# Block attention with a residual LayerNorm: three batch groups, 32-column matmul tiles, and a LayerNorm finish moved from VectorE to GpSimd and TensorE

## The chip, the cores and the metric

One core of one Trainium2 chip. The metric is the device time of one execution, in microseconds, taken as the median of several runs.

## The reference

x is 8 batches of 512 rows of 1024 float32 values (4096 rows, 16 MB). Wk and Wo are 1024 x 1024 float32 (4 MB each). Cut to what matters:

```python
block = x.reshape(8, 8, 64, 1024).sum(2)             # 8 blocks of 64 rows in each batch
keys  = einsum('bnh,kh->bnk', block, Wk)             # 64 keys of 1024
keys  = keys / sqrt(mean(keys**2) + 1e-6) * rms_w
att   = softmax(einsum('bnh,h->bn', keys, cond[1]))  # over the 8 blocks of a batch
attended = einsum('bn,bnh->bh', att, block)          # one vector of 1024 per batch
y     = x + (attended @ Wo.T)[:, None, :]            # the same vector for all 512 rows of a batch
out   = x + (y - mean(y)) / sqrt(var(y) + 1e-6) * gamma + beta
```

The projection of a batch needs the sums over all of that batch's rows, so no row can be finished before the whole of its batch has been read.

## The kernel before, in words

**Layout.** Row r of x lies on partition r // 32, so every partition holds 32 rows of one batch, and a batch has 16 partitions. x is read once, in 16 tiles of two rows per partition (1 MB each, SP queue, L158), and stays in SBUF until it is stored.

**Weights.** Wk and Wo come first, in eight 1 MB tiles that take eight of the 16 x buffers (L127). TensorE transposes them in 128 x 128 pieces (L142) into PSUM, and VectorE and ScalarE take turns at copying the result to `wkT` and `woT` (L149, L151).

**Block sums.** VectorE adds the 32 rows of each partition into `acc` (L161, L164): one addition of 128x1024 per row.

**Attention.** `h_major` (L170) multiplies pieces of `acc` with a block-diagonal matrix, which brings h to the partitions and gives each block two columns. `project` (L180) multiplies that with `wkT`: 16 matmuls of 512 columns, stationary operand 128 columns wide. The profile shows each float32 matmul as two instructions. Scores, softmax and weights follow in a chain of small instructions (L199 to L228). `h_major` and `project` run once more, on the attention weights and `woT`, and leave `proj` in PSUM, on every partition the row of its batch.

**LayerNorm.** For each tile of two rows `stats` makes y = x + proj with its row sum (VectorE, L240), the negative mean `nmu` (VectorE, L245), the sum of squares (ScalarE, L249), and 1 / sqrt by the table's square root and a Newton step of small GpSimd instructions (L95 to L105). `finish` makes z = (y + nmu) * gamma into PSUM (VectorE, L258), x = z * rstd + x (VectorE, L262), x = x + beta (GpSimd, L263), and stores the tile (SP queue, L264). So each row has three VectorE instructions, one ScalarE instruction and one GpSimd instruction of 128x1024.

**Order.** The loops only state the work. A planner gives each engine one fixed order: it plays the program through with its own costs, takes the ready instruction that was stated first, and gives a buffer of a pool to the next tile of that tag when an earlier tile has been released. On the chip each engine then works through its own list in that order.

Of the kernel before, what the change touches and what calls it, by code (L numbers as in the profile page):

```python
# [27 lines left out]
def block_attn_resid_kernel(  # L28
# [42 lines left out]

    def block_diag(name, size, inside, outside):
        t = const.tile([P, P], F32, tag=name, name=name)
        nc.gpsimd.memset(t, inside)
        v = t.rearrange("p (g i) -> p g i", i=size)
        nc.gpsimd.affine_select(
            out=v, in_=v, pattern=[[-size, P // size], [0, size]],
            compare_op=ALU.is_ge, fill=outside, base=0, channel_multiplier=1,
        )
        nc.gpsimd.affine_select(  # L80
            out=v, in_=v, pattern=[[size, P // size], [0, size]],
            compare_op=ALU.is_ge, fill=outside, base=size - 1, channel_multiplier=-1,
        )
        return t

    pair = block_diag("pair", P // (B * 8), 1.0, 0.0)
    batch2 = block_diag("batch2", NB, 2.0, 0.0)
    negmask = block_diag("negmask", NB, 0.0, NEG)
# [3 lines left out]
    def inv_sqrt(eng, ssq, n, name):  # L92
        """1 / sqrt(ssq / H + EPS), with one Newton step after the table's square root."""
        v = small.tile([P, n], F32, tag=f"v{n}", name=f"v_{name}")
        eng.tensor_scalar(v, ssq, 1.0 / H, EPS, ALU.mult, ALU.add)  # L95
        s = small.tile([P, n], F32, tag=f"s{n}", name=f"s_{name}")
        nc.scalar.activation(s, ssq, AF.Sqrt, bias=eps_t, scale=1.0 / H)  # L97
        r = small.tile([P, n], F32, tag=f"r{n}", name=f"r_{name}")
        nc.vector.reciprocal(r, s)
        a = small.tile([P, n], F32, tag=f"a{n}", name=f"a_{name}")  # L100
        eng.tensor_tensor(a, r, r, ALU.mult)
        eng.tensor_tensor(a, a, v, ALU.mult)
        eng.tensor_scalar(a, a, -0.5, 1.5, ALU.mult, ALU.add)
        rr = small.tile([P, n], F32, tag=f"rr{n}", name=f"rr_{name}")
        eng.tensor_tensor(rr, r, a, ALU.mult)  # L105
        return rr

# [1 line left out]
    def vec_tile(src, tag, name):  # L109
        t = tmp.tile([P, H], F32, tag=tag, name=name)  # L110
        nc.scalar.dma_start(out=t, in_=src.rearrange("(o h) -> o h", o=1).to_broadcast([P, H]))
        return t

    q_t = vec_tile(cond[LAYER], "t0", "q_t")
    w_t = vec_tile(rms_w, "t1", "w_t")
    qw = bank_pair("qw", "qw")
    nc.vector.tensor_tensor(flat(qw), q_t, w_t, ALU.mult)  # L117
    g_t = vec_tile(gamma, "t0", "g_t")
    gam = bank_pair("gam", "gam")
    nc.scalar.copy(flat(gam), g_t)  # L120
# [181 lines left out]
```

## Time and profile before

| | us |
|---|---|
| median of 3 runs | 257.05 |
| lowest, highest | 256.84, 262.64 |
| span of the profiled execution, first to last instruction | 260.6 |
| VectorE busy | 176.1 |
| GpSimd busy | 93.3 |
| ScalarE busy | 62.9 |
| TensorE busy with matmuls | 61.4 |

The profiled execution is one execution by itself; its time is told by its span of 260.6 us, from the first to the last instruction, with nothing counted around it. That is 3.5 us above the median of the runs and 2.0 us below the slowest of them. PE is TensorE, PEld its loading of the stationary operand, DVE VectorE, ACT ScalarE, POOL GpSimd, SP the engine that issues most transfers. Busy times of engines overlap, so they don't add up to the span. The granted clock of TensorE is given as a share of 2.4 GHz: 1.00 is 2.4 GHz, 0.50 is 1.2 GHz.

### The profile page before, as it was taken

The page shows a single profiled execution, that of the slowest core. Times are in us where ns is not written, and L with a number is a line of the kernel's source. Part 1 is how long each engine was busy: PE and PEld are TensorE (multiplying, and loading weights), DVE is VectorE, ACT ScalarE, POOL GpSimd, SP SyncE. Part 2 cuts the span into 40 slices and gives each one's busy share as a digit, 9 for nine tenths or more (in the row PEclk, how much of TensorE's full clock was granted, in tenths as well). Part 3 has the DMA queues.
Part 4 walks back from the last instruction along what each step waited for, and adds up shares of the span by engine and source line. Part 5 has one row for each costly group of instructions (what it writes and reads, how often), then busy time and mean ns, then how long its engine had stood idle before and what let it go on. Part 6 is the DMA issues. An engine that isn't in the chain of part 4 may idle for free.

```text
span 260.6 us, 1101 instructions
## 1 busy us (share of the span) xinstructions
PE 61.4 (24%) x226; PEld 39.1 (15%) x226; DVE 176.1 (68%) x220; ACT 62.9 (24%) x105; POOL 93.3 (36%) x129
## 2 busy tenths in 40 slices
PE   0518870000008991589800000000000000000000
PEld 0518660000006440444300000000000000000000
DVE  0111549999991003210199999999999999999950
ACT  0123430000000006200068442234443224444000
POOL 6000000000000000000006768776667876666992
PEclk9999997555555899559955555555555555555555
DMA  6999999999300002000000332233332223333254
GB/s 211 418 408 412 423 419 423 423 423 420 128 0 0 0 0 82 0 3 0 0 0 0 161 141 98 86 161 161 161 161 103 98 122 161 161 161 161 89 214 180
DMA packets 7366, 44.11 MB, mean 169 GB/s; under 512 B 704, under 2 KB 704, under 8 KB 3264
## 3 DMA queue, kind: packets, MB, share of 16 engines
q1 hardware_dynamic: 6784, 41.95, 39.3%
q10 hardware_dynamic: 576, 2.10, 2.3%
q8 instruction: 2, 0.03, 0.0%
q14 instruction: 4, 0.03, 0.0%
HBM read 27.26 MB, written 16.78 MB: 169 GB/s over the span
## 4 chain that ended last, share of the span: by engine, by line
DVE 41%; PE 20%; POOL 16%; ACT 8%; issue 7%; DMA 6%; POOLq 1%; ACTq 0%; DVEq 0%
DVE acc L164 14%; POOL x L263 13%; DVE y L240 8%; DVE z L258 7%; DVE x L262 6%; PE proj L180 6%; PE keys L180 6%; PE pt L142 4%; ACT junk L249 4%; DMA w_t<-n_L_cond_rms_weight_dram 3%; DMA g_t<-in_L_cond_ln_gamma_dram 3%; PE p_attT L170 1%; PE p_blkT L170 1%; DVE woT L149 1%; ACT L97 1%
## 5 line engine op out<-in xcount | busy, mean ns | idle before, releaser
L263 POOL TENSOR_TENSOR x<-x,bet 128x1024 f32<-128x1024 f32 x32 | 74.5, 2350 | 1.5 <-issue 0.5
L95 POOL TENSOR_SCALAR v_y<-ssq 128x2 f32<-128x2 f32 x16 | 3.1, 193 | 154.0 <-ACT junk L249 153.9
L249 ACT ACTIVATE junk<-y,nmu 128x1024 f32<-128x1024 f32 x32 | 36.7, 1147 | 82.2 <-DVE nmu L245 76.6
L240 DVE SCALAR_TENSOR_TENSOR y<-x,proj 128x1024 f32<-128x1024 f32 x32 | 37.5, 1204 | 15.9 <-PE proj L180 15.9
L258 DVE SCALAR_TENSOR_TENSOR z<-y,nmu,gam 128x1024 f32<-128x1024 f32 x32 | 40.7, 1277 | 0.0
L262 DVE SCALAR_TENSOR_TENSOR x<-z,rr_y,x 128x1024 f32<-128x1024 f32 x32 | 39.5, 1270 | 0.0
L164 DVE TENSOR_TENSOR acc<-acc,x 128x1024 f32<-128x1024 f32 x30 | 36.8, 1226 | 1.0
L142 PE MATMUL pt<-ident,w 128*128 128x128 f32 x128 | 20.7, 327 | 17.6 <-DMA w<-in_L_cond_Wk_dram 9.3
L142 PEld LDWEIGHTS pt<-ident,w 128*128 128x128 f32 x128 | 18.0, 170 | 20.1 <-issue 9.3
L180 PE MATMUL proj<-woT,attT 128*128 128x512 f32 x32 | 16.5, 680 | 0.7 <-ACT attT L172 0.7
L180 PE MATMUL keys<-wkT,blkT 128*128 128x512 f32 x32 | 15.9, 660 | 0.7 <-ACT blkT L172 0.7
L149 DVE COPY wkT<-pt 128x1024 f32<-128x1024 f32 x4 | 4.9, 1225 | 14.2 <-PE pt L142 14.2
L170 PE MATMUL p_blkT<-pair,acc 128*128 128x128 f32 x16 | 3.8, 429 | 40.3 <-DVE acc L164 40.3
L201 DVE SCALAR_TENSOR_TENSOR kb<-kb,qw 128x512 f32<-128x512 f32 x2 | 1.4, 686 | 16.8 <-ACT kb L199 16.8
L172 ACT COPY blkT<-p_blkT 128x512 f32<-128x512 f32 x1 | 0.6, 586 | 44.7 <-PE p_blkT L170 44.7
L170 PEld LDWEIGHTS p_blkT<-pair,acc 128*128 128x128 f32 x16 | 3.5, 330 | 40.5 <-issue 40.5
L245 DVE TENSOR_SCALAR nmu<-ysum 128x2 f32<-128x2 f32 x16 | 9.2, 575 | 0.0
L180 PEld LDWEIGHTS proj<-woT,attT 128*128 128x128 f32 x32 | 6.9, 220 | 9.7 <-issue 8.8
L180 PEld LDWEIGHTS keys<-wkT,blkT 128*128 128x128 f32 x32 | 6.8, 216 | 9.3 <-issue 8.3
L149 DVE COPY woT<-pt 128x1024 f32<-128x1024 f32 x4 | 4.9, 1224 | 4.7 <-PE pt L142 4.7
L117 DVE TENSOR_TENSOR qw<-q_t,w_t 128x1024 f32<-128x1024 f32 x1 | 1.2, 1232 | 9.6 <-DMA w_t<-n_L_cond_rms_weight_dram 9.6
L249 ACT ACTIVATION_READ_ACCUMULATOR junk<-y,nmu 128x1 f32 x32 | 6.0, 186 | 0.0
(60 smaller groups left out, 59.5 us busy)
## 6 DMA issues: line engine op xcount, KB each, us to landing
x<-in_x_dram SPq DMA_DIRECT2D x16, 1024.0 KB, 19.8
out_dram<-x SPq DMA_DIRECT2D x16, 1024.0 KB, 3.8
w<-in_L_cond_Wk_dram SPq DMA_DIRECT2D x4, 1024.0 KB, 11.6
w<-in_L_cond_Wo_dram SPq DMA_DIRECT2D x4, 1024.0 KB, 17.5
q_t<-in_cond_dram ACTq DMA_DIRECT2D x1, 512.0 KB, 5.6
w_t<-n_L_cond_rms_weight_dram ACTq DMA_DIRECT2D x1, 512.0 KB, 8.2
g_t<-in_L_cond_ln_gamma_dram ACTq DMA_DIRECT2D x1, 512.0 KB, 7.1
bet<-in_L_cond_ln_beta_dram ACTq DMA_DIRECT2D x1, 512.0 KB, 4.3
```

The lines of the kernel that those rows point to most:

```text
L95: eng.tensor_scalar(v, ssq, 1.0 / H, EPS, ALU.mult, ALU.add)
L142: nc.tensor.transpose(pt[:, c, r * P : (r + 1) * P], stage[which, s][:, r, bass.ts(4 * h4 + c, P)], ident,)
L149: nc.vector.tensor_copy(dst, pt)
L164: nc.vector.tensor_tensor(acc, acc, xx[:, r, :], ALU.add)
L170: nc.tensor.matmul(pb[:, c, :], acc[:, bass.ts(c, P)], rhs, start=True, stop=True)
L180: nc.tensor.matmul(po[:, k, :], lhs[:, c, :], wT[:, c, bass.ts(k, HALF)], start=(c == 0), stop=(c == HC - 1),)
L240: nc.vector.scalar_tensor_tensor(y[:, r, :], xt[t][:, r, :], 1.0, proj, ALU.mult, ALU.add, accum_out=ysum[:, r : r + 1],)
L245: nc.vector.tensor_scalar(nmu, ysum, -1.0 / H, None, ALU.mult)
L249: nc.scalar.activation(junk, y[:, r, :], AF.Square, bias=nmu[:, r : r + 1], accum_out=ssq[:, r : r + 1])
L258: nc.vector.scalar_tensor_tensor(flat(z), y[:, r, :], nmu[:, r : r + 1], flat(gam), ALU.add, ALU.mult)
L262: nc.vector.scalar_tensor_tensor(xr, flat(z), rstd[:, r : r + 1], xr, ALU.mult, ALU.add)
L263: nc.gpsimd.tensor_tensor(xr, xr, bet, ALU.add)
```

## The change

x is worked on in three groups of 2, 2 and 4 batches (`GROUPS`). Each group is spread over all 128 partitions, so groups 0 and 1 have 8 rows per partition (4 tiles of 1 MB), group 2 has 16 (8 tiles). x and the weights share 12 buffers in place of 16: the tiles of group 0 are loaded first, then Wk, Wo, group 1, and group 2, whose tiles take buffers as they come free.

Block sums go from VectorE to TensorE: a 32-column block matrix times 512 columns of x, with the two halves of two rows going to the four 32-partition strips of one PSUM bank. Keys and projection use a stationary operand of 32 columns, with four quarters of the 1024 outputs going to the four strips. Every group has its own block sums, keys, softmax and projection; `spread` matmuls bring the projection to all partitions (`pb`), `pick` matmuls make a small table `tab` of gamma, beta and the projections.

The finish of a row is rewritten as out = y * (1 + gamma * rstd) + (nmu * rstd * gamma + beta - proj): ScalarE makes the factor A, GpSimd the product, TensorE the second bracket as outer products of a transposed table `lt` with `tab` (two matmuls of 512 columns, 6 or fewer used rows of the array), and VectorE adds it. y is written over x. Statistics go by four rows (a quad) in place of two, 1 / sqrt by Ln and Exp. All functions used on ScalarE are in one table, loaded at the start.

```diff
-    for t in range(NT):
...
-            for r in range(RT):
-                nc.vector.tensor_tensor(acc, acc, xx[:, r, :], ALU.add)
...
+GROUPS = (2, 2, 4)
+XBUFS = 12
...
+    xp = ctx.enter_context(tc.tile_pool(name="xp", bufs=XBUFS))
+    work = ctx.enter_context(tc.tile_pool(name="work", bufs=2))
...
+    nc.scalar.preload_act_table_set("natural_log_exp_and_others")
...
+    def block_sums(G):
+        bs = ps.tile([P, HALF], F32, tag="bs", name=f"bs{G['n']}")
+        n = G["rows"]
+        for r in range(n):
+            for h in range(2):
+                j = 2 * (r % 2) + h
+                nc.tensor.matmul(
+                    bs[32 * j : 32 * j + 32, :], blk[G["g"]], G["x"][r // RT][:, r % RT, bass.ts(h, HALF)],
+                    start=(r < 2), stop=(r >= n - 2),
+                )
+        G["bs"] = bs
+
+    def project(lhs, wT, name):
+        po = ps.tile([P, QU], F32, tag="sm", name=name)
+        for c in range(HC):
+            for j in range(4):
+                nc.tensor.matmul(
+                    po[32 * j : 32 * j + 32, :], lhs(c), wT[:, c, bass.ts(j, QU)],
+                    start=(c == 0), stop=(c == HC - 1),
+                )
+        return po
...
+    def attend(G):
...
+        nc.scalar.copy(bss, G["bs"])
+        pb = ps.tile([P, HC, 32], F32, tag="sm", name=f"pblk{n}")
+        for c in range(HC):
+            nc.tensor.matmul(pb[:, c, :], bss[:, bass.ts(c % 4, P)], halves[:, c // 4, :], start=True, stop=True)
+        blkT = chain.tile([P, HC, 32], F32, tag="blkT", name=f"blkT{n}")
+        nc.vector.tensor_copy(blkT, pb)
+
+        keys = project(lambda c: blkT[:, c, :], wkT, f"keys{n}")
...
+        nc.scalar.activation(junk, kb, AF.Square, accum_out=sd[:, 0:1])
+        nc.vector.scalar_tensor_tensor(junk2, kb, 1.0, qw, ALU.mult, ALU.mult, accum_out=sd[:, 1:2])
+
+        sdd = small.tile([P, 2, 32], F32, tag="sdd", name=f"sdd{n}")
+        for s in range(2):
+            nc.vector.tensor_scalar(sdd[:, s, :], diag4, sd[:, s : s + 1], None, ALU.mult)
+        pc = ps.tile([P, 2, 32], F32, tag="sm", name=f"pc{n}")
+        nc.tensor.matmul(flat(pc), ones, flat(sdd), start=True, stop=True)
...
+        nc.scalar.activation(r0, pc[:, 0, :NB], AF.Ln, bias=eps_t, scale=1.0 / H)
+        nc.scalar.activation(r0, r0, AF.Exp, scale=-0.5)
+        nc.vector.tensor_scalar(v, pc[:, 0, :NB], 1.0 / H, EPS, ALU.mult, ALU.add)
+        nc.vector.tensor_tensor(a, r0, r0, ALU.mult)
...
+        wb = chain.tile([P, HC, NB], F32, tag="wb", name=f"wb{n}")
+        nc.vector.tensor_tensor(wb, blkT[:, :, :NB], sc.unsqueeze(1).to_broadcast([P, HC, NB]), ALU.mult)
...
+        att = chain.tile([P, HC, g, 32 // g], F32, tag="att", name=f"att{n}", bufs=2)
+        nc.vector.tensor_copy(att, aT.unsqueeze(3).to_broadcast([P, HC, g, 32 // g]))
+        G["att"] = att
+
+    def proj(G):
+        n, g = G["n"], G["g"]
+        att = G["att"]
+        po = project(lambda c: att[:, c].rearrange("p b m -> p (b m)"), woT, f"po{n}")
...
+        nc.scalar.copy(pr, po)
+        pb = ps.tile([P, 4, QU], F32, tag="pb", name=f"pb{n}")
+        for j in range(4):
+            nc.tensor.matmul(pb[:, j, :], spread[:, j, :], pr, start=True, stop=True)
+        pt = ps.tile([P, 2, QU], F32, tag="sm", name=f"ptab{n}")
+        for k in range(2):
+            nc.tensor.matmul(pt[:, k, :], pick[g][:, k, :], pr, start=True, stop=True)
+        tab = chain.tile([P, HALF], F32, tag="tab", name=f"tab{n}", bufs=2)
+        nc.vector.tensor_tensor(tab, flat(pt), rows, ALU.add)
+        G["pb"], G["tab"] = flat(pb), tab
...
+    def front(G, q):
...
+        xs = G["x"][QT * q : QT * q + QT]
+        for r in range(R):
+            xr = xs[r // RT][:, r % RT, :]
+            nc.vector.scalar_tensor_tensor(
+                xr, xr, 1.0, G["pb"], ALU.mult, ALU.add, accum_out=ysum[:, r : r + 1]
+            )
+        nc.gpsimd.tensor_scalar(nmu, ysum, -1.0 / H, 0.0, ALU.mult, ALU.add)
+        for r in range(R):
+            junk = work.tile([P, H], F32, tag="A", name=f"sq{n}_{q}_{r}")
+            nc.scalar.activation(
+                junk, xs[r // RT][:, r % RT, :], AF.Square, bias=nmu[:, r : r + 1], accum_out=ssq[:, r : r + 1]
+            )
...
+        nc.scalar.activation(r0, ssq, AF.Ln, bias=eps_t, scale=1.0 / H)
+        nc.scalar.activation(r0, r0, AF.Exp, scale=-0.5)
+        nc.gpsimd.tensor_scalar(v, ssq, 1.0 / H, EPS, ALU.mult, ALU.add)
+        nc.gpsimd.tensor_tensor(a, r0, r0, ALU.mult)
+        nc.gpsimd.tensor_tensor(a, a, v, ALU.mult)
+        nc.gpsimd.tensor_scalar(a, a, -0.5, 1.5, ALU.mult, ALU.add)
+        nc.gpsimd.tensor_tensor(rs, a, r0, ALU.mult)
...
+        for k in range(QT):
+            st = stat[G["g"]][k]
+            nc.gpsimd.tensor_tensor(
+                st[:, :, :, 0],
+                nmu[:, RT * k : RT * k + RT].unsqueeze(2).to_broadcast([P, RT, 2]),
+                rs[:, RT * k : RT * k + RT].unsqueeze(2).to_broadcast([P, RT, 2]),
+                ALU.mult,
+            )
+            pl = ps.tile([P, P], F32, tag="sm", name=f"pl{n}_{q}_{k}")
+            nc.tensor.transpose(pl, st.rearrange("p r i k -> p (r i k)"), ident)
+            lt = small.tile([P, P], F32, tag="lt", name=f"lt{n}_{q}_{k}")
+            nc.vector.tensor_copy(lt, pl)
+            lts.append(lt)
+        G["st", q] = (rs, lts)
...
+    def back(G, q):
...
+        for r in range(QT * RT):
+            t = QT * q + r // RT
+            xr = G["x"][t][:, r % RT, :]
+            A = work.tile([P, H], F32, tag="A", name=f"A{n}_{q}_{r}")
+            nc.scalar.activation(A, gam, AF.Identity, bias=1.0, scale=rs[:, r : r + 1])
+            nc.gpsimd.tensor_tensor(xr, xr, A, ALU.mult)
+            b = ps.tile([P, 2, HALF], F32, tag=f"b{r % 2}", name=f"b{n}_{q}_{r}")
+            for i in range(2):
+                lo = 32 * (2 * (r % RT) + i)
+                nc.tensor.matmul(
+                    b[:, i, :], lts[r // RT][lo : lo + K, :], G["tab"][lo : lo + K, :], start=True, stop=True
+                )
+            nc.vector.tensor_tensor(xr, xr, flat(b), ALU.add)
+            if r % RT == RT - 1:
+                nc.sync.dma_start(out=G["out_v"][t], in_=G["x"][t])
...
+    load_x(groups[0])
+    load_w(0, wk)
+    load_w(1, wo)
+    late_vectors()
+    block_sums(groups[0])
+    transpose_w(0, wkT)
+    attend(groups[0])
+    transpose_w(1, woT)
+    proj(groups[0])
+
+    todo = [(G, q) for G in groups for q in range(G["tiles"] // QT)]
+    ready = 1
+    load_x(groups[1])
+    block_sums(groups[1])
+    attend(groups[1])
+    pending = []
+    for G, q in todo:
+        if q == 0 and G["n"] > 0:
+            proj(G)
+        if q == 0 and G["n"] + 1 < len(groups) and G["n"] + 1 > ready:
+            ready = G["n"] + 1
+            load_x(groups[ready])
+            block_sums(groups[ready])
+            attend(groups[ready])
+        front(G, q)
+        pending.append((G, q))
+        if len(pending) > 1:
+            back(*pending.pop(0))
+    while pending:
+        back(*pending.pop(0))
```

## Rows read from the trace of the kernel before

**Rows 1.** Page, part 2: 40 equal slices of 6.5 us, each digit a tenth.

```profile
DVE  0111549999991003210199999999999999999950
...
PEclk9999997555555899559955555555555555555555
...
DMA  6999999999300002000000332233332223333254
```

**Rows 2.** Busy by stage: stretch, length, then PE, PEld, DVE, ACT, POOL; clock, DMA, GB/s.

```profile
18.00:38.00 20.00, 15.67 (x107) 13.92 (x108) 7.35 (x6) 9.07 (x9) 0.00 (x0) 1.00 1.02 416
...
38.00:78.00 40.00, 0.28 (x3) 0.05 (x1) 38.65 (x32) 0.00 (x0) 0.00 (x0) 0.56 0.74 307
...
78.00:83.00 5.00, 3.75 (x16) 3.49 (x16) 0.47 (x1) 0.54 (x1) 0.00 (x0) 0.50 0.00 0
...
83.00:99.00 16.00, 15.90 (x32) 6.80 (x32) 0.69 (x1) 0.05 (x1) 0.00 (x0) 0.88 0.00 0
...
99.00:108.00 9.00, 0.77 (x3) 0.50 (x2) 3.89 (x18) 5.91 (x12) 0.00 (x0) 0.78 0.19 59
...
113.00:129.00 16.00, 16.00 (x32) 6.51 (x31) 0.27 (x1) 0.00 (x0) 0.00 (x0) 0.85 0.00 1
...
146.00:254.00 108.00, 0.00 (x0) 0.00 (x0) 104.99 (x132) 35.89 (x65) 81.01 (x99) 0.50 0.35 145
```

**Rows 3.** Groups by line: engine, out<-in, count | busy us, mean ns | idle before, releaser.

```profile
L263 POOL TENSOR_TENSOR x<-x,bet 128x1024 f32<-128x1024 f32 x32 | 74.5, 2350 | 1.5 <-issue 0.5
...
L258 DVE SCALAR_TENSOR_TENSOR z<-y,nmu,gam 128x1024 f32<-128x1024 f32 x32 | 40.7, 1277 | 0.0
...
L262 DVE SCALAR_TENSOR_TENSOR x<-z,rr_y,x 128x1024 f32<-128x1024 f32 x32 | 39.5, 1270 | 0.0
...
L240 DVE SCALAR_TENSOR_TENSOR y<-x,proj 128x1024 f32<-128x1024 f32 x32 | 37.5, 1204 | 15.9 <-PE proj L180 15.9
...
L249 ACT ACTIVATE junk<-y,nmu 128x1024 f32<-128x1024 f32 x32 | 36.7, 1147 | 82.2 <-DVE nmu L245 76.6 <-POOL a_y L102 5.1
...
L102 POOL TENSOR_TENSOR a_y<-a_y,v_y 128x2 f32<-128x2 f32 x16 | 3.1, 197 | 1.3
...
L97 ACT ACT_TABLE_LOAD x2 | 2.6, 1283 | 0.3 <-DVE kss L206 0.3
```

**Rows 4.** Instructions in time order, 129 to 135 us: start, us, engine, line.

```profile
129.15 1.22 DVE L240 SCALAR_TENSOR_TENSOR y<-x,proj 128x1024 f32<-128x1024 f32 x1 [15.88 <-PE proj L180]
...
130.29 1.22 DVE L240 SCALAR_TENSOR_TENSOR y<-x,proj 128x1024 f32<-128x1024 f32 x1
...
132.58 0.17 DVE L245 TENSOR_SCALAR nmu<-ysum 128x2 f32<-128x2 f32 x1
...
132.78 1.15 ACT L249 ACTIVATE junk<-y,nmu 128x1024 f32<-128x1024 f32 x1 [20.23 <-DVE nmu L245]
...
134.05 1.15 ACT L249 ACTIVATE junk<-y,nmu 128x1024 f32<-128x1024 f32 x1
```

**Rows 5.** The same view, 202 to 256 us.

```profile
202.52 4.66 POOL L263 TENSOR_TENSOR x<-x,bet 128x1024 f32<-128x1024 f32 x2
...
206.58 0.63 DVE L245 TENSOR_SCALAR nmu<-ysum 128x2 f32<-128x2 f32 x1
...
210.18 4.66 POOL L263 TENSOR_TENSOR x<-x,bet 128x1024 f32<-128x1024 f32 x2
...
246.39 9.24 POOL L263 TENSOR_TENSOR x<-x,bet 128x1024 f32<-128x1024 f32 x4
```

**Rows 6.** TensorE weight loads of the keys in time order, 84 to 89 us.

```profile
84.97 0.34 PEld L180 LDWEIGHTS keys<-wkT,blkT 128*128 128x128 f32 x1 [0.52 <-issue]
...
88.54 0.19 PEld L180 LDWEIGHTS keys<-wkT,blkT 128*128 128x128 f32 x1 [0.24 <-issue]
```

**Rows 7.** First transposes, in time order.

```profile
9.31 3.65 PE L142 MATMUL pt<-ident,w 128*128 128x128 f32 x16 [9.31 <-DMA w<-in_L_cond_Wk_dram]
```

**Rows 8.** Page, part 6: DMA issues, KB each, median us to landing.

```profile
out_dram<-x SPq DMA_DIRECT2D x16, 1024.0 KB, 3.8
```

More of the change, by code (lines that the diff above doesn't have):

```diff
@@ L79, in block_diag @@
         )
         nc.gpsimd.affine_select(
-            out=v, in_=v, pattern=[[size, P // size], [0, size]],
-            compare_op=ALU.is_ge, fill=outside, base=size - 1, channel_multiplier=-1,
-        )
[L84 to L88, printed above, removed]
-    eps_t = const.tile([P, 1], F32, tag="eps", name="eps_t")
-    nc.gpsimd.memset(eps_t, EPS)
[L92 to L106, printed above, removed]
@@ L109, in vec_tile @@
[L109 to L120, printed above, removed]
+            out=v, in_=v, pattern=[[-s, n] for s, n in pattern], compare_op=ALU.is_ge, fill=0.0,
@@ new lines, in band, with spots @@
+            base=width - 1, channel_multiplier=-1,
+        )
+    def spots(v, pattern, base):
+        nc.gpsimd.affine_select(
+            out=v, in_=v, pattern=pattern, compare_op=ALU.not_equal, fill=1.0, base=base, channel_multiplier=1
+        )
+    blk = {}
+    for g in sorted(set(GROUPS)):
+        t = const.tile([P, 32], F32, tag=f"blk{g}", name=f"blk{g}")
+        nc.gpsimd.memset(t, 1.0)
+        band(t, [[-(16 // g), 32]], 16 // g)
+        blk[g] = t
+    halves = const.tile([P, 2, 32], F32, tag="halves", name="halves")
@@ new lines, in block_attn_resid_kernel, with late_vectors @@
+    nc.gpsimd.memset(rows, 0.0)
+    def late_vectors():
+        nc.scalar.dma_start(out=gam, in_=gamma.rearrange("(o h) -> o h", o=1).to_broadcast([P, H]))
+        for k, v in ((0, gamma), (1, beta)):
+            h = v.rearrange("(i o h) -> i o h", i=2, o=1)
+            for q in range(4):
+                nc.scalar.dma_start(out=rows[32 * q + k : 32 * q + k + 1, :], in_=h[q % 2])
+    xf = x.rearrange("b s h -> (b s) h")
+    of = out.rearrange("b s h -> (b s) h")
+    groups = []
+    at = 0
@@ new lines, in block_attn_resid_kernel, with load_x @@
+    for n, g in enumerate(GROUPS):
+        lo, hi = at * S, (at + g) * S
+        groups.append(dict(
+            n=n, g=g, rows=4 * g, tiles=4 * g // RT,
+            x_v=xf[lo:hi].rearrange("(p t r) h -> t p r h", p=P, r=RT),
+            out_v=of[lo:hi].rearrange("(p t r) h -> t p r h", p=P, r=RT),
+        ))
+        at += g
+    def load_x(G):
+        G["x"] = []
+        for t in range(G["tiles"]):
+            xx = xp.tile([P, RT, H], F32, tag="x", name=f"x{G['n']}_{t}")
+            nc.sync.dma_start(out=xx, in_=G["x_v"][t])
+            G["x"].append(xx)
@@ L184, in project @@
         return po
-    blkT = h_major(pair, "p0", "blkT")
-    keys = project(blkT, wkT, "p1", "keys")
-    wk_stack.close()
-    late = ctx.enter_context(tc.tile_pool(name="late", bufs=1))
-    bet = late.tile([P, H], F32, tag="bet", name="bet")
-    nc.scalar.dma_start(out=bet, in_=beta.rearrange("(o h) -> o h", o=1).to_broadcast([P, H]))
-    kb = tmp.tile([P, 2, HALF], F32, tag="t0", name="kb")
-    ssq2 = small.tile([P, 2], F32, tag="ssq2", name="ssq2")
-    dot2 = small.tile([P, 2], F32, tag="dot2", name="dot2")
@@ L198, in block_attn_resid_kernel @@
-    for k in range(2):
-        nc.scalar.copy(kb[:, k, :], keys[:, k, :])
-        nc.scalar.activation(keys[:, k, :], keys[:, k, :], AF.Square, accum_out=ssq2[:, k : k + 1])
-        nc.vector.scalar_tensor_tensor(
-            kb[:, k, :], kb[:, k, :], 1.0, qw[:, k, :], ALU.mult, ALU.mult,
-            accum_out=dot2[:, k : k + 1],
-        )
-    kss = small.tile([P, 1], F32, tag="kss", name="kss")
-    nc.vector.tensor_tensor(kss, ssq2[:, 0:1], ssq2[:, 1:2], ALU.add)
-    dot = small.tile([P, 1], F32, tag="dot", name="dot")
@@ L208, in block_attn_resid_kernel @@
-    nc.vector.tensor_tensor(dot, dot2[:, 0:1], dot2[:, 1:2], ALU.add)
-    rrms = inv_sqrt(nc.vector, kss, 1, "keys")
-    score = small.tile([P, 1], F32, tag="score", name="score")
-    nc.vector.tensor_tensor(score, dot, rrms, ALU.mult)
-    diag = const.tile([P, P], F32, tag="diag", name="diag")
-    nc.vector.tensor_scalar(diag, ident, score, None, ALU.mult)
-    pbc = ps.tile([P, P], F32, tag="p0", name="pbc")
-    nc.tensor.matmul(pbc, ones, diag, start=True, stop=True)
-    sm = const.tile([P, P], F32, tag="sm", name="sm")
```

193 lines of the change are left out of this document (98 added, 95 removed).

## The prediction

> **What bounds the kernel now.** I read the profile from the outside in: the slices of the page, the busy times by stage, then single instructions. The slices show four phases one behind the other: transfers alone, VectorE full, VectorE nearly empty, VectorE full to the end [rows 1]. The stages put numbers to it [rows 2]. Until about 38 us the weights load and are transposed at 416 GB/s. From 38 to 78 VectorE is busy 38.65 of 40 us with the row sums. From 78 to 129 the attention runs with little beside it: 3.75 us for the block sums, 15.9 for the keys, 9 for the softmax chain, 16 for the projection. From 129 VectorE streams the rows; it is busy 104.99 of 108 us between 146 and 254, GpSimd 81.01. One row costs it three instructions (1.204, 1.277 and 1.270 us [rows 3]), and a tile of two rows takes 210.18 - 202.52 = 7.66 us [rows 5], 3.83 a row. The last GpSimd addition ends at 246.39 + 9.24 = 255.63, and the span of 260.6 has a tail of 5.0 us behind it, the last store with 3.8 us of it [rows 5, 8]. So the path is loads, row sums, attention, streaming, in series; nothing of the last three lies beside another.
>
> **The change, part by part.** My sum is on the profiled execution's time base, 260.6 us from first to last instruction, which is 3.5 above the median of 257.05; I do not scale for that.
>
> *VectorE.* The 38.65 us of row sums leave. Per row two of the three streaming instructions stay: about 1.15 (starts 129.15 and 130.29 [rows 4]) and about 1.27 [rows 3], 2.4 in place of 3.83, so 77 us for 32 rows. VectorE is no longer the bound.
>
> *ScalarE.* Per row a square, 1.27 from start to start [rows 4], and now the factor A, about 1.15 by the same row without its accumulator: 2.4. The table loads of 1.28 us [rows 3] leave the path.
>
> *GpSimd.* Its addition of 2.35 us [rows 3] becomes a product of the same shape: 2.35 a row, 9.4 a quad of four rows. Seven small ones per quad behind the squares, 0.2 us each [rows 3], about 2 us with the gaps. This is the longest stream, 32 x 2.35 = 75 us, and no other engine takes it over.
>
> *The shared pool.* A and the scratch of the squares share a pool of two buffers. While GpSimd works on one A and the next waits, no square can start. When one comes free, the squares of the next quad, stated first, go ahead: 4 x 1.27 + 0.6 for Ln and Exp + 1.15 for the next A = 6.85 us, of which a running product covers 2.35. I take a stall of 4.5 us of GpSimd per quad, the small instructions inside it, wherever a quad's squares did not run ahead. Bounds: 0, if the squares slip in between, and 6.85.
>
> *32-column tiles.* No row has them. A keys matmul of 512 columns is two instructions, 0.34 + 0.52 = 0.86 us apart at a granted clock of 0.5, 0.19 + 0.24 = 0.43 at 1.00 [rows 6]. A projection becomes 32 matmuls of 256 columns. If the four strips run one behind the other, that is 32 x 0.43 = 13.7 us, as now, and three times in place of once. If four run together, 8 x 0.43 = 3.4. Between: four together, but their eight weight loads a round, a quarter of 0.19 us each, are not hidden: 8 x (0.43 + 0.38) = 6.5 us. I take 6.5, since in these rows a load never adds to the matmul beside it but nothing says so for strips. Block sums per 1 MB tile likewise: 3.43, 0.86, and 1.24 taken, below the 2.5 us in which a tile lands at 416 GB/s. The Trainium skill, "TensorE: Matmul & The Clock Gate" (Part 3: Packing small matmuls), gives 2.38 times the speed for three column tiles; three times for four would be an estimate of 4.6 us a projection and a sum 8 us lower. No run here shows it yet.
>
> *Start.* x of group 0 (4.2 MB) goes ahead of the weights: 8.4 MB to the end of Wk is 20 us at 416 GB/s, from about 3 us, so 23.5; transposes and copies behind it, 27. In the kernel now the first weight tile is there at 9.31 [rows 7]; that wait is now used for block sums. Keys 6.5, with the transposes of Wo between them 8; the chain 7 (9 now, less the table loads); projection 6.5; its copy and spread (four matmuls of 0.43) 2.3. The projection of group 0 stands at about 52 us, in place of 129.
>
> *First quads.* Four additions with `pb` (4.9 with `nmu`), eight squares (10.2, since the second quad's come first), 0.6 and 1.15: 17 us to the first product, at 69. Group 0: 9.4 + 4.5 + 9.4, to 92. Group 1 follows to about 120; its attention lies beside group 0.
>
> *Group 2.* Only 12 buffers: its last four tiles wait for the stores of group 0. Last product 92, addition 1.2, store 3.8 [rows 8], load taken at the same 3.8: 101. Then in series: block sums 1.2, copy 0.6, transposing matmuls 3.75 as in the stage from 78 [rows 2], copy 0.6, keys 6.5, chain 7, projection 6.5, spread 2.3: 28.5, to 129.5. To this I add two delays. `nmu` on VectorE takes 0.17 us alone but 0.63 while GpSimd works, ending just when GpSimd's pair ends at 207.18 [rows 4, 5]; eight small instructions of the chain have only operands in SBUF, so 0 to 8 x 2.35 = 19 us. I take 2, since GpSimd runs out of work at about 120. TensorE has outer products of group 1 between: two matmuls of 512 columns per row are 1.72 us at full clock, 3.43 at half; I take 4 us in all. That is 135.5. The Trainium skill, "GPSIMD Engine Reference" (Specifications), names contention with VectorE for a 2-port mode and for two SBUF inputs; `nmu` has one input, so the second half is not shown here.
>
> *End.* 17 us to group 2's first product, 152.5; four quads 4 x 9.4 + 2 x 4.5 = 46.6, to 199; last addition 1.2, tail 5. **Sum: 205 us.** GpSimd idles from about 120 to 152 in it: group 2's attention is what is late next.
>
> **Rivals.**
>
> *Group 2 is ready in time.* If its attention does not open a gap, GpSimd streams through: 69 + 32 x 2.35 + 6 x 4.5 + 6.2 = 177 us. For it: each term of the 28.5 us was taken above its lower bound, and four overlapping strips save 3.1 at each projection. Against it: the reload behind the stores is a true dependence, and 32 us have to vanish.
>
> *Half clock.* The granted clock was 0.50 in the stage from 78 to 83, when TensorE had long been idle, and still 0.88 as a mean of the keys [rows 2]. If the short bursts of this kernel never raise it, four projections on the path cost 6.5 more each: 231 us. Outer products at 3.43 a row make 13.7 a quad, about GpSimd's 9.4 + 4.5, so they add little. For it: gaps of several microseconds in each chain. Against it: in the transposing stage, busy with small gaps, the clock stays at 1.00 [rows 2].
>
> *The strips do not run together.* Then the change does not do what its tiles say, and TensorE is the bound. Ahead of group 2's spread it has 64 matmuls of block sums (0.86 each, 55 us), six projections (82), outer products of groups 0 and 1 (27.5), 128 transposes (19, from 15.67 for 107 [rows 2]) and about 19 of spreads and transposing matmuls: 202 us, after 9 of waiting and with 7 of chain at the end, 218. With 17 + 46.6 + 6.2 behind: about **285 us, slower**. Only the first 137 shrink with a speed-up s of strips: at s = 1.28 the time equals the present one, at 1.22 it is 2% slower. For it: no row of the trace shows strips at work. Against it: only that four strips read and write apart.
>
> **How the numbers follow.** Forecast 60% (205; its own range 185 to 222), group 2 ready in time 15% (177), half clock 14% (231), strips in series 11% (285). The range leaves out about half of the second case below and the last with a little of the third above: 178 to 240. Within 2% (251.9 to 262.2, about what a measurement here can tell from no change) lie s near 1.28 and a half clock with all waits on GpSimd's port, 4%; slower 8%, the rest of the last case; faster 88%.
>
> **What would show it.** Right: `pb` of group 0 done at 45 to 58 us; 32 products of about 2.35 us on GpSimd, in quads with a gap of some microseconds; a long GpSimd gap ahead of group 2, ended by a chain that goes back through keys, block sums, a load of x and a store of group 0; four matmuls of a projection with starts close together. Wrong: matmuls of strips starting 0.43 us apart, or TensorE busy over 80% in mid-span; no gap on GpSimd; a granted clock of 0.5 through the streaming; products slower than 2.35 us; ScalarE or VectorE without idle time while GpSimd waits; or block sums of group 2 at the head of TensorE's list, waiting for x while outer products stand behind them.

## The result, and the profile after

The changed kernel takes **246.59 us** (median of 4 runs, 244.43 to 247.58); the kernel before took 259.78 beside it (median of 4). The ratio is 0.959, 95% interval 0.952 to 0.966: faster, by 4%. Two of the four runs before took about 257 us and two about 262.6, and this ratio, like those below, compares only the faster runs of each kernel. Forecast were 205 us and a range of 178 to 240. The sign was right and the size was not: the profiled execution spans 244.5 us, 39.5 more than the sum.

Page, part 1, of the changed kernel (busy us, share of the span, instructions) and lines of part 2 (40 slices of 6.1 us, in tenths):

```profile
PE 156.2 (64%) x874; PEld 68.8 (28%) x874; DVE 103.9 (42%) x178; ACT 91.8 (38%) x145; POOL 95.0 (39%) x147
...
DVE  0000444828546608834000156169586363244551
...
POOL 8500000000229500097492000000892948929990
PEclk9999999999796579855555865696555555555555
```

VectorE is no longer full to the end [rows 1]. GpSimd, forecast as the longest stream, works in three islands with two holes of 3 and 6 slices between. Busy time by stage of the changed kernel (columns as in [rows 2]):

```profile
72.00:92.00 20.00, 16.23 (x97) 6.39 (x97) 8.48 (x15) 4.17 (x7) 10.46 (x10) 0.66 0.41 155
92.00:128.00 36.00, 12.35 (x54) 3.23 (x52) 14.70 (x21) 18.70 (x28) 19.51 (x22) 0.64 0.38 148
128.00:161.00 33.00, 27.94 (x180) 13.43 (x177) 9.92 (x26) 2.59 (x8) 1.98 (x3) 0.67 0.16 64
...
188.00:236.00 48.00, 31.12 (x66) 8.66 (x62) 20.87 (x27) 26.85 (x37) 38.53 (x37) 0.50 0.37 155
```

From 72 to 128, where groups 0 and 1 were to stream without a break, GpSimd is busy 29.97 of 56 us. GpSimd's own instructions show where it stops (start, us, engine, line, idle time before and what ended it):

```profile
72.24 2.36 POOL L350 TENSOR_TENSOR x<-x,A 128x1024 f32<-128x1024 f32 x1 [1.17 <-ACT A L349]
...
78.29 4.66 POOL L350 TENSOR_TENSOR x<-x,A 128x1024 f32<-128x1024 f32 x2
...
98.21 0.20 POOL L308 TENSOR_SCALAR nmu<-ysum 128x4 f32<-128x4 f32 x1 [15.26 <-DVE x L305]
...
104.19 4.66 POOL L350 TENSOR_TENSOR x<-x,A 128x1024 f32<-128x1024 f32 x2 [0.57 <-ACT A L349]
...
112.43 2.35 POOL L350 TENSOR_TENSOR x<-x,A 128x1024 f32<-128x1024 f32 x1
...
142.16 0.20 POOL L328 TENSOR_TENSOR stat<-nmu,rs 128x4 f32<-128x4 f32 x1 [12.59 <-PE pl L335]
...
172.66 4.66 POOL L350 TENSOR_TENSOR x<-x,A 128x1024 f32<-128x1024 f32 x2 [0.57 <-ACT A L349]
...
187.91 2.35 POOL L350 TENSOR_TENSOR x<-x,A 128x1024 f32<-128x1024 f32 x1 [0.85 <-ACT A L349]
```

Group 0's first quad ends at 78.29 + 4.66 = 82.95; its second starts at 104.19, 21.2 us later. In between stands `nmu` of **group 1**, which waits for group 1's first additions. The same happens at the next change: group 1's second quad (172.66) runs only after `nmu` of group 2. ScalarE's rows in that hole say why (same columns):

```profile
78.06 1.15 ACT L349 ACTIVATE A<-gam,rs 128x1024 f32<-128x1024 f32 x1 [2.29 <-POOL x L350]
89.93 0.37 ACT L283 COPY pr<-po 128x256 f32<-128x256 f32 x1 [10.72 <-PE po L218]
98.44 1.15 ACT L311 ACTIVATE sq<-x,nmu 128x1024 f32<-128x1024 f32 x1 [8.13 <-POOL nmu L308]
...
102.98 1.13 ACT L349 ACTIVATE A<-gam,rs 128x1024 f32<-128x1024 f32 x1
```

After the last `A` of group 0's first quad ScalarE stands idle for 18.85 us in all, 10.72 before the copy of group 1's projection and 8.13 before group 1's squares. Only behind these comes the next `A`, the one that group 0's second quad needs. The factors wait for the whole entry of the next group.

TensorE's bursts are right in kind, and better than taken (same columns; a stated float32 matmul is two instructions here):

```profile
47.01 3.66 PE L218 MATMUL po<-woT,att 128*32 128x256 f32 x64 [1.02 <-DVE att L275]
51.44 1.99 PE L286 MATMUL pb<-pr,spread 128*128 128x256 f32 x8
...
126.35 1.94 PE L208 MATMUL bs<-x,blk 128*32 128x512 f32 x8 [5.36 <-DMA x<-in_x_dram]
...
133.13 5.13 PE L218 MATMUL keys<-wkT,blkT 128*32 128x256 f32 x64 [0.52 <-DVE blkT L233]
139.65 0.43 PE L248 MATMUL pc<-sdd,ones 128*128 128x64 f32 x2 [1.39 <-DVE sdd L246]
141.72 0.30 PE L335 MATMUL pl<-ident,stat 128*128 128x128 f32 x1 [1.63 <-DVE cs L260]
...
152.78 5.54 PE L218 MATMUL po<-woT,att 128*32 128x256 f32 x64
159.30 1.99 PE L286 MATMUL pb<-pr,spread 128*128 128x256 f32 x8
```

A projection takes 3.66 us, and 5.1 to 5.7 further on, where the granted clock lies lower (0.66 as the mean of 72 to 92, 0.67 of 128 to 161); it took 15.9 before [rows 2]. Group 0's spread projection is done at 53.4 (forecast 52).

Where the forecast and the runs part, on one clock (us from the span's start; e3, e7 and e12 are experiments below: two edits, then one more, then one more again):

| | forecast | after | e3 | e7 | e12 |
|---|---|---|---|---|---|
| first product of group 0 | 69 | 72.2 | 73.2 | 74.8 | 75.7 |
| last product of group 0 done | 92 | 114.8 | 93.1 | 94.7 | 95.6 |
| last block sums of group 2 done | 102.2 | 128.3 | 108.4 | 111.4 | 112.5 |
| its spread projection done | 135.5 | 161.3 | 164.1 | 154.5 | 148.5 |
| first product of group 2 | 152.5 | 187.9 | 178.7 | 169.1 | 163.2 |
| last product done | 199 | 238.2 | 224.3 | 214.6 | 208.7 |
| end of the span | 205 | 244.5 | 230.5 | 220.9 | 215.0 |

Differences down a column give the steps: group 0's products took 42.6 us in place of 23; from block sums to spread projection 33.0 in place of 33.3; from there to group 2's first product 26.6 in place of 17; the four quads 50.3 in place of 46.6; the tail 6.3 in place of 6.2.

### The profile page after: what moved, and what is told of

It is laid out like the page before. It is cut to its first block, busy times and chain, and to the rows that moved or that the text cites. A ratio compares the mean times of both kernels' runs of the same rounds, so it can differ in the third digit from the quotient of the medians.

```text
span 244.5 us, 2478 instructions
## 1 busy us (share of the span) xinstructions
PE 156.2 (64%) x874; PEld 68.8 (28%) x874; DVE 103.9 (42%) x178; ACT 91.8 (38%) x145; POOL 95.0 (39%) x147
## 4 chain that ended last, share of the span: by engine, by line
PE 35%; POOL 22%; ACT 12%; issue 10%; DMA 10%; DVE 8%; POOLq 1%; ACTq 0%; DVEq 0%
POOL x L350 19%; PE keys L218 7%; ACT sq L311 7%; PE b L354 6%; PE po L218 6%; DMA x<-in_x_dram 5%; PE pt L188 4%; PE pblk L231 4%; PE bs L208 3%; DVE x L305 3%; DMA qw<-in_cond_dram 3%; ACT A L349 3%; PE pb L286 2%; DMA out_dram<-x 2%; DVE x L357 2%
## 5 line engine op out<-in xcount | busy, mean ns | idle before, releaser
L354 PE MATMUL b<-tab,lt 4*128 4x512 f32 (+1 forms) x128 | 62.4, 1056 | 30.0 <-DVE x L357 29.9
L350 POOL TENSOR_TENSOR x<-x,A 128x1024 f32<-128x1024 f32 x32 | 74.7, 2350 | 5.4 <-ACT A L349 5.4
L357 DVE TENSOR_TENSOR x<-x,b 128x1024 f32<-128x1024 f32 x32 | 38.8, 1219 | 38.8 <-POOL x L350 26.2
L311 ACT ACTIVATE sq<-x,nmu 128x1024 f32<-128x1024 f32 x32 | 36.5, 1140 | 31.4 <-POOL nmu L308 17.3
L305 DVE SCALAR_TENSOR_TENSOR x<-x,pb 128x1024 f32<-128x1024 f32 x32 | 37.4, 1215 | 19.8 <-PE pb L286 19.8
L349 ACT ACTIVATE A<-gam,rs 128x1024 f32<-128x1024 f32 x32 | 36.6, 1142 | 23.2 <-POOL x L350 21.1
L208 PE MATMUL bs<-x,blk 128*32 128x512 f32 x128 | 23.1, 771 | 22.7 <-DMA x<-in_x_dram 16.5
L354 PEld LDWEIGHTS b<-tab,lt 4*128 4x128 f32 (+1 forms) x128 | 16.4, 285 | 54.5 <-DVE x L357 47.8
L218 PE MATMUL keys<-wkT,blkT 128*32 128x256 f32 x192 | 16.4, 462 | 1.7 <-DVE blkT L233 1.0
L188 PE MATMUL pt<-ident,w 128*128 128x128 f32 x128 | 16.9, 293 | 0.0
L218 PE MATMUL po<-woT,att 128*32 128x256 f32 x192 | 14.9, 479 | 1.0 <-DVE att L275 1.0
L320 POOL TENSOR_SCALAR v<-ssq 128x4 f32<-128x4 f32 x8 | 1.6, 194 | 33.3 <-ACT sq L311 33.3
```

What stands on the lines that cost most here:

```text
L188: nc.tensor.transpose(pt[:, c, r * P : (r + 1) * P], stage[which, s][:, r, bass.ts(4 * h4 + c, P)], ident)
L208: nc.tensor.matmul(bs[32 * j : 32 * j + 32, :], blk[G["g"]], G["x"][r // RT][:, r % RT, bass.ts(h, HALF)], start=(r < 2), stop=(r >= n - 2),)
L218: nc.tensor.matmul(po[32 * j : 32 * j + 32, :], lhs(c), wT[:, c, bass.ts(j, QU)], start=(c == 0), stop=(c == HC - 1),)
L305: nc.vector.scalar_tensor_tensor(xr, xr, 1.0, G["pb"], ALU.mult, ALU.add, accum_out=ysum[:, r : r + 1])
L311: nc.scalar.activation(junk, xs[r // RT][:, r % RT, :], AF.Square, bias=nmu[:, r : r + 1], accum_out=ssq[:, r : r + 1])
L349: nc.scalar.activation(A, gam, AF.Identity, bias=1.0, scale=rs[:, r : r + 1])
```

## Experiments

**Theory.** The hole at a group's change is the order in which `A` and the squares' scratch, one tag with two buffers, are handed out: in stated order, and the next group's projection and first additions are stated ahead of the finish of the last quad. **Rivals.** Two buffers are simply too few; TensorE at half clock; a group's own chain is that long.

**e1_drain**: the last quad of a group is finished ahead of the next group's projection.

```diff
         if q == 0 and G["n"] > 0:
+            while pending:
+                back(*pending.pop(0))
             proj(G)
```

> The finishes of a group's last quad are stated ahead of the next group's projection; nothing else changes. Theory 'stated order' (ScalarE's list puts the next group's four squares ahead of the factors A of the last quad, so GpSimd waits for the next group's projection): the GpSimd gap of 21 us behind group 0's first quad falls to under 6 us, group 0's last product ends near 97 us in place of 115, group 1 is finished before group 2's projection, and the span is 210 to 222 us. Rival 'TensorE' (the half clock and the outer products and projections in TensorE's own list set the gap): gap and span stay within 2% of 244.5. Rival 'too few buffers' (two buffers for A and the squares are too few wherever they meet): the gap stays, span over 235.

Measured: 237.96 us, ratio 0.926 (0.924 to 0.929). GpSimd in this run (same columns as above, as in all lists below):

```profile
71.50 2.37 POOL L350 TENSOR_TENSOR x<-x,A 128x1024 f32<-128x1024 f32 x1 [1.17 <-ACT A L349]
...
77.56 13.93 POOL L350 TENSOR_TENSOR x<-x,A 128x1024 f32<-128x1024 f32 x6
104.18 0.19 POOL L308 TENSOR_SCALAR nmu<-ysum 128x4 f32<-128x4 f32 x1 [12.69 <-DVE x L305]
...
115.96 4.68 POOL L350 TENSOR_TENSOR x<-x,A 128x1024 f32<-128x1024 f32 x2 [0.84 <-ACT A L349]
```

The hole inside group 0 is gone: its products end at 91.49, the 92 of the forecast. But only 8.6 us come back, since group 1's first product is at 115.96 and group 2's spread projection is no earlier than in the changed kernel (162.5 for 161.3).

**e2_scratch**: the squares get a buffer of their own, nothing else.

```diff
-            junk = work.tile([P, H], F32, tag="A", ...)
+            junk = work.tile([P, H], F32, tag="S", ..., bufs=1)
```

> The squares write to a scratch buffer of their own, so A has both buffers of its pool; the stated order stays. Theory 'stated order': the gap came about because the shared pool hands out buffers in the stated order, so with a pool of its own A no longer stands behind the next group's squares, and the gap behind group 0's first quad closes to under 6 us; span 212 to 225 us. 'Too few buffers' expects the same here. 'TensorE' expects 240 to 246.

Measured: 238.93 us, ratio 0.929 (0.927 to 0.932). Group 0's six last products run in one piece here too (79.62 to 93.56), with the statements in their old order. So it is the shared tag that ties `A` to the next group's squares, and not TensorE at half clock that opens the hole: this edit leaves TensorE's work as it was.

**e3_both**: both edits. 

> Both edits: finishes of the last quad stated ahead of the next projection, and a scratch buffer of its own for the squares. 'Stated order': boundary gaps closed as with either edit, and the stall of each quad (15.2 us from quad to quad where four products need 9.4) falls to 10 to 13 us as well, so 198 to 214 us. 'TensorE': 240 to 246, since an outer product row at half clock takes 2.1 us and four rows with the transposes about 10.

Measured: 232.75 us, ratio 0.905 (0.901 to 0.908). In these three runs the hole closed as expected, and in e3 the quads of group 2 come 12.1 us apart in place of 15.2, as expected too. The times were all missed: e3 gains 22 us at group 0's last product and 14 at the end.

**e4_bufs3**: the shared tag with three buffers in place of two. 

> The shared pool of A and squares has three buffers in place of two, as much memory as the own scratch takes; stated order and sharing stay. 'Stated order': ScalarE's list still has the next group's squares ahead of the last quad's A, the gap of about 21 us stays, the quads gain at most 2 us each, and the span is 232 to 246 us. 'Too few buffers': as good as the own scratch, 212 to 225 us.

Measured: 243.65 us, ratio 0.948 (0.941 to 0.956). ScalarE's list has the same order, and the hole stays:

```profile
77.65 4.65 POOL L350 TENSOR_TENSOR x<-x,A 128x1024 f32<-128x1024 f32 x2
97.58 0.19 POOL L308 TENSOR_SCALAR nmu<-ysum 128x4 f32<-128x4 f32 x1 [15.29 <-DVE x L305]
...
103.57 4.67 POOL L350 TENSOR_TENSOR x<-x,A 128x1024 f32<-128x1024 f32 x2 [0.57 <-ACT A L349]
```

It is the order; a third buffer does not help.

**What was late next.** With the hole closed, group 2's block sums are done 20 us earlier (108.4), yet its spread projection is at 164.1: the chain takes 55.7 us in place of 33.0. It now lies beside group 1's products. VectorE in e3:

```profile
129.69 0.19 DVE L256 TENSOR_SCALAR cv<-pc 128x32 f32<-128x32 f32 x1 [1.10 <-ACT cr L254]
130.84 2.37 DVE L257 TENSOR_TENSOR ca<-cr 128x32 f32<-128x32 f32 x1 [0.96 <-ACT cr L255]
133.25 2.28 DVE L258 SCALAR_TENSOR_TENSOR ca<-ca,cv 128x32 f32<-128x32 f32 x1
135.56 0.19 DVE L259 SCALAR_TENSOR_TENSOR ca<-ca,cr 128x32 f32<-128x32 f32 x1
...
137.74 0.17 DVE L267 TENSOR_REDUCE es<-cs 128x4 f32<-128x32 f32 x1
137.94 0.18 DVE L268 RECIPROCAL es<-es 128x4 f32<-128x4 f32 x1
138.16 1.95 DVE L269 TENSOR_TENSOR cs<-cs,es 128x32 f32<-128x32 f32 x1
```

And GpSimd in the same stretch of e3:

```profile
126.21 9.26 POOL L350 TENSOR_TENSOR x<-x,A 128x1024 f32<-128x1024 f32 x4
...
137.72 2.34 POOL L350 TENSOR_TENSOR x<-x,A 128x1024 f32<-128x1024 f32 x1
```

Four products from 126.21 to 135.47 end about every 2.31 us, at 128.5, 130.8, 133.2 and 135.5. L257 ends at 133.21, L258 at 135.53: each small operation is over when the running product is. L259, in GpSimd's pause, takes 0.19. Inside the next product (137.72 to 140.06) L267 and L268, which read one tensor in SBUF, take 0.17 and 0.18; L269, which reads two, ends with it, at 140.11. And in the changed kernel and e3 alike the transposes `pl` of group 1 came only behind group 2's `pc`, with outer products of group 1 between that and group 2's projection (142.7 to 152.8 in the changed kernel; in e3 from 145.2, behind the projection's first two instructions, to 155.3).

**e5_bank**: `pl` takes the bank of the block sums in place of the one it shares with `keys`, `pc`, `po` and the table.

```diff
-            pl = ps.tile([P, P], F32, tag="sm", ...)
+            pl = ps.tile([P, P], F32, tag="bs", ...)
```

> Only edit against the changed kernel: the transposed statistics (pl) take the bank of the block sums instead of the bank that keys, pc, po and the table share. Theory 'bank': group 1's transposes wait for the shared bank until group 2's pc is done (12.59 us of wait on POOL's statistics), and the outer products then stand ahead of group 2's projection (142.5 to 152.8 us). With a bank of its own they run while group 2's keys are being made: group 2's spread projection 6 to 9 us earlier (152 to 155 instead of 161.3), total 237 to 242. Rival 'paced by GpSimd': the outer products only follow the products of group 1 and the wait moves into them: spread projection of group 2 at 159 to 163, total 244 to 248.

Measured: 242.82 us, ratio 0.941 (0.928 to 0.954); this is the median of 241.50, 241.92, 243.71 and one execution of 292.15, on which the profile fell and which the ratio leaves out. **e13_bank_look** is the same kernel once more, for its profile. 

> The bank edit alone once more, for a profile of it. Theory 'bank': group 2's spread projection 6 to 9 us earlier than 161.3. Rival 'paced by GpSimd': 159 to 163.

Measured: 242.46 us, one run. TensorE there:

```profile
125.09 1.94 PE L208 MATMUL bs<-x,blk 128*32 128x512 f32 x8 [5.34 <-DMA x<-in_x_dram]
...
131.16 0.45 PE L335 MATMUL pl<-ident,stat 128*128 128x128 f32 x1
...
148.76 5.64 PE L218 MATMUL po<-woT,att 128*32 128x256 f32 x64
155.38 1.99 PE L286 MATMUL pb<-pr,spread 128*128 128x256 f32 x8
```

The first `pl` goes ahead of `pc`, and the spread projection is done at 157.4 in place of 161.3: 3.9 us, where 6 to 9 were expected; the total lies just above the 237 to 242 given for the bank.

**e9_s_bank** (bank and e2) and **e7_all3** (bank and e3):

> The bank edit on top of the own scratch buffer of the squares (238.93 without it). Theory 'bank': 6 to 9 us less, 229 to 233, group 2's spread projection at 153 to 156 instead of 162.0. Rival 'paced by GpSimd': 237 to 241, spread projection still at 160 to 164.

> The bank edit on top of both earlier edits: own scratch, and the last quad of a group finished ahead of the next group's projection (232.75 without it). Here group 1's last products are stated ahead of group 2's projection, so that projection cannot start before they are done. Theory 'bank': group 1's products run closer together (they took 116.5 to about 152 for 19 us of work), spread projection of group 2 at 152 to 157 instead of 164.2, total 221 to 226. Rival 'paced by GpSimd and ScalarE's list': total 231 to 235, spread projection at 162 to 166.

Measured: 228.74 us, ratio 0.885 (0.870 to 0.900), and **222.98 us, ratio 0.865 (0.853 to 0.877)**. The totals came about as expected of the bank, 10 us less in each, but only e7 shows it where it was expected: its chain from block sums to spread projection is 43.1 us, 12.6 less than in e3. In e9 the spread projection stays at 161.4 (162.0 without the bank), and the gain is in group 2's quads, 12.1 us apart in place of 15.2. e3 has 12.1 without the bank. In e2 `nmu` of group 2's second quad stands on GpSimd behind the third product of the first (182.59), so its squares start only at 182.82. In e3 and e9 it stands ahead of the first product (174.08 and 174.15), and the squares run beside the products. Why the planner orders e2's list differently stays open.

**e12_narrow_g1**: e7, with group 1's product on 8 of its 1,024 columns. The rest of that product is left out.

```diff
-            nc.gpsimd.tensor_tensor(xr, xr, A, ALU.mult)
+            w = 8 if n == 1 else H
+            nc.gpsimd.tensor_tensor(xr[:, :w], xr[:, :w], A[:, :w], ALU.mult)
```

> On top of the three edits (222.98): group 1's product on GpSimd covers 8 of 1,024 columns, the rest of group 1's product is left out. Theory 'group 2's chain is held by group 1's streaming': the small VectorE operations of the chain (1.0 to 2.3 us each beside GpSimd) fall back to 0.2 us, the outer products and additions of group 1 no longer wait for products, and the spread projection of group 2 moves from 154 to 139 to 145 (its x landed at 110, 28.5 us of chain and 2 to 4 of clock behind it): total 208 to 214. Rival 'the chain's own latency at half clock': spread projection at 150 to 153, total 219 to 223.

Measured: 216.44 us, ratio 0.840 (0.836 to 0.844). Two of the chain's operations, in e7:

```profile
135.91 1.26 DVE L258 SCALAR_TENSOR_TENSOR ca<-ca,cv 128x32 f32<-128x32 f32 x1
137.20 2.26 DVE L259 SCALAR_TENSOR_TENSOR ca<-ca,cr 128x32 f32<-128x32 f32 x1
```

The same two in e12:

```profile
132.60 0.18 DVE L258 SCALAR_TENSOR_TENSOR ca<-ca,cv 128x32 f32<-128x32 f32 x1
132.82 0.19 DVE L259 SCALAR_TENSOR_TENSOR ca<-ca,cr 128x32 f32<-128x32 f32 x1
```

The chain takes 36.0 us, so 7.1 of e7's 43.1 belong to group 1's products, by the waiting small operations and by the additions and outer products that wait for them, together. The spread projection comes at 148.5, past the 139 to 145 expected, and the total lies between the 208 to 214 of the theory and the 219 to 223 of the rival: the copy of the block sums still stands 3 us behind group 1's squares on ScalarE.

**e8_all3_g2222**: e7 with four groups of two batches. 

> The same three edits with four groups of two batches: the third group needs no tile that is loaded behind group 0's stores, only the fourth does, at the price of a fourth projection, chain and group change. Theory 'late group': what holds the end is that four batches wait for one late chain (x landed at 106, spread projection at 164); half of them freed of it, GpSimd goes on with the third group at about 150 and the fourth group's chain lies beside that: 212 to 224. Rival 'group change': each change of group leaves GpSimd idle by about 20 us (91 to 116 and 150 to 179 with three groups) whatever is ready, and a third change adds 15 to 20 us: 240 to 252.

Measured: 240.92 us (median of 4, 236.23 to 241.68), beside 261.66 of the kernel before; the lowest is 13 us above e7's median. GpSimd in this run:

```profile
131.80 9.32 POOL L350 TENSOR_TENSOR x<-x,A 128x1024 f32<-128x1024 f32 x4 [0.82 <-ACT A L349]
...
167.79 2.35 POOL L350 TENSOR_TENSOR x<-x,A 128x1024 f32<-128x1024 f32 x1 [3.25 <-ACT A L349]
...
179.79 9.29 POOL L350 TENSOR_TENSOR x<-x,A 128x1024 f32<-128x1024 f32 x4 [0.82 <-ACT A L349]
...
211.39 4.68 POOL L350 TENSOR_TENSOR x<-x,A 128x1024 f32<-128x1024 f32 x2 [0.83 <-ACT A L349]
```

Each change leaves GpSimd without a product for 22 to 27 us (141.1 to 167.8, 189.1 to 211.4). The times lie at and below the lower end of the rival's 240 to 252, far from the theory's 212 to 224. The rival is the nearer one: a third change costs more than the early half brings.

**e11_proj_first**: e7, with group 1's projection ahead of the finish of group 0's last quad.

```diff
+            if G["n"] == 1:
+                proj(G)
             while pending:
                 back(*pending.pop(0))
-            proj(G)
+            if G["n"] > 1:
+                proj(G)
```

> On top of the three edits (222.98): group 1's projection and spread are stated ahead of the finishes of group 0's last quad (group 2's stay behind group 1's, as there). Its attention is ready at about 70 and the spread's bank is free when group 0's last first-addition is done (about 77). Theory 'group change is latency, not work': GpSimd's gap between group 0's last product (94.6) and group 1's first (118.9) is po 6.4, copy and spread 2.7, additions, squares and statistics 16; with po and spread beside group 0's products it shrinks from 24 to 10 to 17 us, and as group 2's chain follows its own reload, 4 to 10 us of it reach the end: 213 to 219. Rival 'engines are full there': the additions and squares of group 1 only push group 0's products and additions back, the gap moves, total 221 to 226.

Measured: 222.92 us, ratio 0.866 (0.860 to 0.872), as e7. The gap between group 0's last product and group 1's first does shrink, from 24.2 us to 18.6 (95.3 to 114.0), but group 2's spread projection is at 155.5, no earlier than in e7 (154.5): shortening the gap between groups 0 and 1 does not reach the end.

**e14_bss_dve**: e7, with the copy of group 2's block sums on VectorE.

```diff
-        nc.scalar.copy(bss, G["bs"])
+        (nc.vector.tensor_copy if n == 2 else nc.scalar.copy)(bss, G["bs"])
```

> On top of the three edits (222.98): the copy of group 2's block sums goes to VectorE instead of ScalarE. There the sums were done at 111.4 and the copy began at 116.05, between ScalarE's squares; VectorE is done with group 1's first additions at 112.5. Theory 'group 2's chain is set by ScalarE's order at its head': the copy at 112.6, the whole chain 3 to 3.5 us earlier, spread projection of group 2 at 150 to 151 instead of 154, total 219 to 220.5. Rival 'it lies behind group 1's products anyway' (VectorE's small operations and the outer products wait for those): spread projection at 153 to 154.5, total 222 to 224.

Measured: 221.57 us (6 runs, 218.56 to 223.39), ratio 0.856 (0.850 to 0.862): not separable from e7, and between the totals of the two expectations. The copy starts 3.7 us earlier (112.31 for 116.05), the spread projection is done 0.8 earlier (153.7). Group 1's outer products stand between (139.4 to 145.1 on TensorE, just ahead of the projection), as the rival has it.

So e7, three edits on the changed kernel, takes 0.865 of the time before, and beats both kernels.

## Why the prediction failed

**Right.** *Strips run together*, so the rival of strips in series is out; 6.5 us a projection was taken; 3.7 to 5.7 were seen in the changed kernel, up to 6.5 in the experiments. The Trainium skill, "TensorE: Matmul & The Clock Gate" (Part 3: Packing small matmuls), gives 2.38 times for three column tiles; here four strips bring 13.7 / 3.66 = 3.7 times against the serial sum of the prediction. *GpSimd's product* takes 2350 ns, as taken from [rows 3], 74.7 us for 32. *Group 0's spread projection* came at 53.4 for 52, but with luck: the terms given for it add to 50.8, TensorE could start the projection only at 47.0 where they give 42, and projection and spread then took 6.4 us for 8.8. *Group 2's chain* is in series and took 33.0 us for 33.3 where no product of GpSimd ran beside it (7.3 of them a wait behind group 1's outer products, where 2 + 4 had been added for ports and outer products); it goes back through a load and a store of group 0, as forecast (5.5 us of store and 4.8 of load on the chain that ended last, where 3.8 were taken for each). *The tail* was 6.3 for 6.2.

**The step that failed** is the one on the shared pool: "I take a stall of 4.5 us of GpSimd per quad", with bounds of 0 and 6.85 (its terms make 6.83), and after it "Group 0: 9.4 + 4.5 + 9.4, to 92". Within a group the stall is about that: two of group 2's quads come 15.2 us apart, 5.8 over four products, and all four took 50.3 us for 46.6. But a group's **last** quad has the next group's squares ahead of its factors, and those wait for that group's projection, copy, spread and first additions. The stall there is 21.2 us, three times the upper bound. The bound was worked out from the durations of what stands ahead in the list, not from when these can start. e1 and e2 close the hole by two different edits, e4 shows that a third buffer does not. This cost 19.6 us at group 0, and 9.6 at group 2's entry, where group 1's second quad had to pass first. With 3.2 before the first product, 3.3 in the reload and 3.7 in the last quads that makes up the 39 us.

**The second miss was hidden by the first.** "I take 2, since GpSimd runs out of work at about 120" puts group 2's chain into GpSimd's quiet, though by the forecast's own terms the small operations of that chain lie at about 114 to 121, beside group 1's products. In the changed kernel it was quiet, but only because the hole had pushed group 1's second quad behind the chain. Where the hole is closed, the chain meets group 1's products and costs 55.7 us (e3), 43.1 without the shared bank (e7), 36.0 without the products too (e12). The forecast's 33.3 with its 2 + 4 us for GpSimd's port and outer products is short of e3 by 22. So e3 gives back 14 of the 39.5 us, the bank in e7 another 10, and the narrow products of e12 another 6.

**What is left.** e12 still ends 10 us after the forecast: its last block sums are done 10.3 us later than forecast, 3.6 by group 0's last product and 6.7 by the reload behind the stores (16.9 us from that product to the sums, for 10.2). The other steps of that column differ from the forecast by under 3 us each. Why the first product is late by 3 to 7 us was not tried.

**Rivals.** *Half clock* names a real thing: the granted clock is 0.50, the lower of its two levels (1.2 GHz), from 188 to 236, with gaps in TensorE's work all through, and projections at the mixed clocks up to 161 cost 1.5 to 2.1 us more each. In the streaming it is not the bound: TensorE is busy 31.12 of 48 us there and GpSimd 38.53, and in e3 and e9 the quads come 12.1 us apart at the same 0.50. What it costs elsewhere was not isolated; no edit here changes the clock. *Group 2 ready in time* did not happen in any run. Three signs that were set for being wrong did appear, the clock of 0.50, TensorE busy 27.94 of 33 us from 128 to 161, and block sums of group 2 waiting 5.36 us for x at the head of TensorE's list; none of them is shown to set the time. In the case of *strips in series* the terms given add to 288 us, not 285.

## What to carry to other kernels

Where two uses share a buffer tag, or one PSUM bank, and each engine works through a fixed list, ask of the last user before a phase change what is stated ahead of it and **when that can start**; the stall is that wait, not the durations in the list. A hole of that kind can also be what keeps a later chain undisturbed, so close it together with what the chain will then meet: here 14 us came from the order and the scratch, and 10 more from one bank tag. A fourth group did not pay here, where each change of group left GpSimd without a product for 22 to 27 us.

## What the hardware showed

In e3 small VectorE operations with two operands in SBUF end when GpSimd's running product ends (0.19 us alone, up to 2.37 beside it). Those that read PSUM do not notice it (L256 0.19 us at 129.69, in the middle of a product; additions of x and PSUM 1.22 us throughout), nor do a reduction and a reciprocal of one tensor in SBUF (L267 and L268). The Trainium skill, "GPSIMD Engine Reference" (Specifications), names contention for VectorE instructions in a 2-port mode or with two SBUF inputs, and "SBUF — State Buffer" (Terms) says that the shared port pair is held for a full instruction; the rows agree with both.

Four 32-column strips take 3.66 us for 64 instructions of 256 columns at a granted clock of 1.00 (47 to 50.7 us), 0.06 us each, against 3.4 worked out for four together without weight loads: the loads add about 0.2 us, where 0.38 us for each of eight rounds had been taken for them.
